# Cross-attention on one core: seven products for three more batches, softmax sums accumulated by ScalarE

## The chip, the cores and the metric

The kernel runs on one core of a Trainium2 chip. Its engines work side by side, each on its own queue in order: TensorE (PE) multiplies matrices and writes PSUM, VectorE (DVE), ScalarE (ACT) and GpSimd (POOL) work on tiles of 128 partitions, and SyncE (SP) issues the transfers. The metric is the time of one execution on the device, in microseconds (us); lower is better.

## The reference

There are 16 batches of 256 queries of width 256 (`x`) and 77 keys of width 192 (`ctx`), 8 heads of width 256, all in fp32. What is computed:

```python
Q = (x @ Wq).reshape(B, -1, 8, 256).transpose(0, 2, 1, 3)
K = (ctx @ Wk)...; V = (ctx @ Wv)...             # the same shape, 77 keys
attn = softmax(where(mask, Q @ K^T / 16, -inf))  # over the 77 keys
out = concat_heads(attn @ V) @ Wo + x
return (out - mean) / sqrt(var + 1e-5) * gamma + beta   # layer norm over 256
```

## The kernel before, in words

The projections are folded into the weights. A first part (to 56.67 us) forms G = Wq Wk^T and U = Wv Wo for each head. After that queries and values are never projected: scores are x times `a` = G ctx^T, and the output is the softmax weights times `vw` = ctx U.

The main loop runs over `b` from -1 to 14. Each turn takes in a new batch (`new`, b + 1), finishes the attention of `now` (b), and normalises and stores `old` (b - 1). A batch is two tiles of 128 queries. The order on each engine is written out by hand in the loop body; no scheduler changes it. In a turn:

- TensorE: `scores` of the new batch (L313, two tiles, two PSUM banks each), `prepare_vw` of the new batch (L241, L252), `prepare_a` for one of the four places of the next group of four batches (L199, L213; only while there is a next group, that is up to the turn in which batch 11 enters), then the attention of batch b.
- VectorE: `shift` (L328 adds the mask's bias to the scores, L335 takes the negated maximum `top`), later `den` (L348, the sum of the exponentials) and `rden` (L350), the statistics of the old batch (`finish`, L484, L487), `invert` (L502, 1/std), `normalise` (L524, L527), `turn` (L366, turns the weights p in blocks of 32), turning of the next group's x (L175; in the turns in which the third and fourth batch of a group enter), `add_product` (L476, adds the product in PSUM to x).
- ScalarE: `exponential` (L342, eight activations a tile, with `top` as bias), a Sqrt for the standard deviation (`spread`, L495, with a table load), the copies of `vw` and `a` out of PSUM (L859), the copy of the seven products' bank (L452), and a first Exp (L865 or L886) that brings the Exp table back.
- GpSimd: `weigh` (L356, p = e times rden), `differences` (L392), `add_seven` (L462), `sums` (L409 to L412), and for tiles that are put `aside` part of normalising (L506, L521, L522).
- SyncE: stores of each finished batch (L535), loads of the next group's x.

The attention of a batch, two tiles of weights times `vw`, is a product of 2 x 2 blocks for the first 64 keys. For batches 0 to 10 (`NS = B - GB - 1`, which is 11) it is done with seven products in place of eight (`seven`, L429): GpSimd forms `differences` of the blocks of vw and `sums` of the blocks of turned p beforehand, TensorE multiplies, and `add_seven` adds the products up. For batches 11 to 15 it is done directly (`attend`, L378). The remaining 13 keys are an ordinary product in both. The branch at L862 takes the seven products, L883 the direct attention of batches 11 to 13 (there the first of two tiles is normalised aside, on ScalarE and GpSimd), L892 that of batch 14; what follows the loop is batch 15.

PSUM has eight banks, given out in rotation; a bank is free again when VectorE or ScalarE has read it. The tiles `s` and `e` have two buffers each, `ts` and `ss` two, turned p four, `vw` three.

Of the kernel before, what the change touches and what calls it, by code (L numbers as in the profile page):

```python
# [8 lines left out]
F32 = mybir.dt.float32  # L9
I32 = mybir.dt.int32  # L10
AF = mybir.ActivationFunctionType
ALU = mybir.AluOpType
AX = mybir.AxisListType
PSUM = bass.MemoryType.PSUM

P = 128
H = 8
D = 256
EPS = 1e-05
GB = 4  # L20
# [33 lines left out]
def kernel(  # L54
# [13 lines left out]
    nc = tc.nc  # L68
    B, S, DI = x.shape
# [4 lines left out]
    NG = B // GB  # L74
# [3 lines left out]
    NF = H // 2  # L78
# [18 lines left out]
    st = ctx.enter_context(tc.tile_pool(name="st", bufs=4))  # L97
# [4 lines left out]
    eps = const.tile([P, 1], F32, tag="eps", name="eps")  # L102
# [6 lines left out]
    NH = DI // 2 // BK  # L109
    uA = const.tile([P, 5, NH, NF, BK], F32, tag="uA", name="uA")  # L110
    uB = const.tile([P, 5, NH, NF, BK], F32, tag="uB", name="uB")
    NS = B - GB - 1

    def of_e(u, e):
        return u[:, 3 - 2 * e : 5 - 2 * e].rearrange("p q n i c -> p (q n) i c")
# [10 lines left out]
    bias = const.tile([P, B, S2], F32, tag="bias", name="bias")  # L126
# [45 lines left out]
    def transpose_x(g, j):  # L172

        cols = xT_of[g][:, j * NM : (j + 2) * NM]
        nc.vector.transpose(cols, cols)  # L175
# [161 lines left out]

    def exponential(t):
        e = sp.tile([P, H, S2], F32, tag="e", name=f"e_{t}")
        s, top = s_of.pop(t)  # L340
        for h in range(H):
            nc.scalar.activation(e[:, h], s[:, h], AF.Exp, bias=top[:, h : h + 1])  # L342
        e_of[t] = e

    def weigh(t):
        e = e_of.pop(t)
        den = st.tile([P, H], F32, tag="den", name=f"den_{t}")
        nc.vector.tensor_reduce(den, e, AX.X, ALU.add)  # L348
        rden = st.tile([P, H], F32, tag="rden", name=f"rden_{t}")
        nc.vector.reciprocal(rden, den)  # L350
        p = p_ring[t % 2]
        e_mh = e.rearrange("p (m h) k -> p m h k", h=2)
        rden_mh = rden.rearrange("p (m h) -> p m h", h=2)
        for cols, keys in ((slice(2 * KM), slice(KM)), (slice(2 * KM, 2 * S2), slice(KM, None))):
            part = p[:, :, cols].rearrange("p m (h k) -> p m h k", h=2)
            nc.gpsimd.tensor_tensor(  # L356
                part,
                e_mh[:, :, :, keys],
                rden_mh.unsqueeze(3).to_broadcast(list(part.shape)),
                ALU.mult,  # L360
            )

    def turn(t):
        p = p_ring[t % 2]
        pT_of[t] = turned.tile([P, NF + 1, NM, BK], F32, tag="pT", name=f"pT_{t}", bufs=4)
        nc.vector.transpose(  # L366
            pT_of[t].rearrange("p n m q -> p m n q"),
            p.rearrange("p m (n k) -> p m n k", k=BK),
        )

    ps_of, s_of, e_of, pT_of, po_of = {}, {}, {}, {}, {}
# [13 lines left out]
        po_of[t] = po  # L385


    def differences(b):

        vw = vw_of[b].rearrange("p q k d -> p q (k d)")  # L390
        ts = vwp.tile([P, 3, 2, P], F32, tag="ts", name=f"ts_{b}", bufs=2)
        nc.gpsimd.tensor_tensor(  # L392
            ts.rearrange("p q k d -> p q (k d)"),
            vw[:, 1:4],
            vw[:, 0:1].to_broadcast([P, 3, 2 * P]),
            ALU.subtract,
        )
        ts_of[b] = ts
# [75 lines left out]
    def add_product(t):  # L474
        y = xg_of[t // GT][:, t % GT, :]
        nc.vector.tensor_tensor(y, po_of.pop(t), y, ALU.add)  # L476

    def finish(t):
        if t in po_of:
            add_product(t)  # L480
        g, j = t // GT, t % GT
        y = xg_of[g][:, j, :]
        bn = st.tile([P, 6], F32, tag="bn", name=f"bn_{t}")
        nc.vector.bn_stats(bn, y)  # L484
        if j == 0:
            mv_of[g] = st.tile([P, GT, 2], F32, tag="mv", name=f"mv_{g}", bufs=2)
        nc.vector.bn_aggr(mv_of[g][:, j, :], bn)  # L487
# [3 lines left out]
    def spread(first, last):  # L491

        g, lo, hi = first // GT, first % GT, (last - 1) % GT + 1
        std = st.tile([P, GT], F32, tag="std", name=f"std_{first}")
        nc.scalar.activation(std[:, lo:hi], mv_of[g][:, lo:hi, 1], AF.Sqrt, bias=eps)  # L495
        std_of[first, last] = std

    def invert(first, last, aside=()):

        g, lo, hi = first // GT, first % GT, (last - 1) % GT + 1  # L500
        rstd = st.tile([P, GT], F32, tag="rstd", name=f"rstd_{first}")
        nc.vector.reciprocal(rstd[:, lo:hi], std_of.pop((first, last))[:, lo:hi])  # L502
        if aside:
            less = st.tile([P, GT], F32, tag="less", name=f"less_{first}")
            for j in (t % GT for t in aside):
                nc.gpsimd.tensor_scalar(  # L506
                    less[:, j : j + 1], mv_of[g][:, j, 0:1], rstd[:, j : j + 1], -1.0,
                    ALU.mult, ALU.mult,
                )
        for t in range(first, last):  # L510
            j = slice(t % GT, t % GT + 1)
            rstd_of[t] = rstd[:, j], less[:, j] if aside else None

    def normalise(t, aside=False):

        g, j = t // GT, t % GT
        rstd, less = rstd_of.pop(t)
        y = xg_of[g][:, j, :]
        if aside:
            nc.scalar.activation(y, y, AF.Identity, bias=less, scale=rstd)  # L520
            nc.gpsimd.tensor_tensor(y, y, gam, ALU.mult)  # L521
            nc.gpsimd.tensor_tensor(y, y, bet, ALU.add)  # L522
        else:
            nc.vector.scalar_tensor_tensor(  # L524
                y, y, mv_of[g][:, j, 0:1], gam, ALU.subtract, ALU.mult
            )
            nc.vector.scalar_tensor_tensor(y, y, rstd, bet, ALU.mult, ALU.add)  # L527
        if t >= NT - QT:
            nc.sync.dma_start(out_rows[:, t, :], y)
            return  # L530
        done.append(t)
        if t ^ 1 in done:
            t |= 1
            j |= 1
            nc.sync.dma_start(  # L535
                out_rows[:, t + 1 - QT : t + 1, :], xg_of[g][:, j + 1 - QT : j + 1, :]
            )
# [291 lines left out]
    for b in range(-1, B - 1):  # L829
        old = range(max(b - 1, 0) * QT, b * QT)  # L830
        now = range(max(b, 0) * QT, (b + 1) * QT)
        new = range((b + 1) * QT, (b + 2) * QT)
        for t in new:
            scores(t)
        for t in new:
            shift(t)
        for n in range(0, 2) if b < 0 else range(b + 2, min(b + 3, B // 2)):
            turn_last(n)
        g, n = (b + 1) // GB + 1, (b + 1) % GB
        work = [prepare_vw(b + 1)]  # L840
        if g < NG:
            work.append(prepare_a(g, (n,)))
            if n == 0:
                load_xT(g)
                load_x(g)
        for part_A, _, _ in work:
            part_A()
        for _, part_B, _ in work:
            part_B()
        for i, t in enumerate(new):  # L850
            exponential(t)
            if old:
                finish(old[i])
            weigh(t)
        if old:
            spread(old[0], old[-1] + 1)
        for _, _, copies in work:
            for dst, src in copies():
                nc.scalar.copy(dst, src)  # L859
        if b + 1 < NS:  # L860
            differences(b + 1)
        if b < NS:  # L862
            if now:
                seven(b)
            nc.scalar.activation(warm, eps, AF.Exp)  # L865
            if old:
                invert(old[0], old[-1] + 1)
                normalise(old[0])
            for t in new:
                turn(t)  # L870
            if n >= NF - 2:
                for j in range((n - NF + 2) * GT // 2, (n - NF + 3) * GT // 2, 2):
                    transpose_x(g, j)
            if old:
                normalise(old[1])
            if now:
                add_seven(b)
            if b + 1 < NS:
                sums(b + 1)
            continue  # L880
        for t in now:
            attend(t)
        if b < B - 2:  # L883
            invert(old[0], old[-1] + 1, aside=old[:1])
            normalise(old[0], aside=True)
            nc.scalar.activation(warm, eps, AF.Exp)  # L886
            turn(new[0])
            normalise(old[1])
            turn(new[1])
            for t in now:  # L890
                add_product(t)
        else:  # L892
            turn(new[0])
            invert(old[0], old[-1] + 1, aside=old)
            for t in old:
                normalise(t, aside=True)
            turn(new[1])
            for t in now:
                finish(t)
            spread(now[0], now[-1] + 1)  # L900


    for t in new:
# [43 lines left out]
```

## Time and profile before

| | |
|---|---|
| median of 3 runs | 282.15 us (280.95 to 282.51) |
| the profiled execution | 280.93 us, span 279.2 us, mean TensorE clock 0.993 |
| busy PE / DVE / ACT / POOL | 269.7 / 206.0 / 166.4 / 168.2 us |
| exponentials L342 | 256 of 346 ns, 67.1 us busy |
| sums of exponentials L348 | 32 of 772 ns, 24.7 us |
| differences L392 on GpSimd | 11 of 1995 ns, 21.9 us |
| main loop begins, last product ends | 56.67 us, about 271.9 us |

How to read it: the span goes from the first to the last instruction of the profiled execution; the rest of that execution's time lies around it. Rows of groups give busy time and the mean of one; neighbours on an engine overlap, so the busy time of a group can be less than its count times its mean. "Idle before" names what released the engine after it had stood still. The chain is the work that ended last, followed back from the last instruction.

### The profile page before, as it was taken

How to read it: one execution, taken by the hardware profiler on the slowest of the kernel's cores; microseconds unless marked ns; L12 is line 12 of the kernel's file. 1: busy time of each engine (PE TensorE's matmuls, PEld its weight loads, DVE VectorE, ACT ScalarE, POOL GpSimd, SP SyncE). 2: the span in 40 equal slices, each digit the busy share in tenths (PEclk: the TensorE clock that was granted, in tenths of full speed). 3: DMA queues.
4: the chain of work that ended last, by engine and by line, in shares of the span. 5: the costliest groups of instructions: out<-in, count | busy, mean ns of one | idle time of the engine just before them, and what ended most of it. 6: DMA issues, size and time to landing. Idle time of an engine off the chain costs nothing.

```text
span 279.2 us, 13274 instructions
## 1 busy us (share of the span) xinstructions
PE 269.7 (97%) x5924; PEld 194.8 (70%) x5924; DVE 206.0 (74%) x421; ACT 166.4 (60%) x447; POOL 168.2 (60%) x228
## 2 busy tenths in 40 slices
PE   8899999999999999999999999999999999999990
PEld 7756599976495959595959585858686858476550
DVE  0353953777738989878788888787787878788873
ACT  2303222146738586868676767777776766978751
POOL 1000069947677777787877777777778445426183
PEclk9999999999999999999999999999999999999997
DMA  6997999920000101940100009501001011010112
GB/s 198 247 223 154 305 262 236 225 82 4 2 6 2 40 5 41 190 155 4 42 2 30 16 25 190 172 5 42 4 5 40 2 42 38 4 41 2 40 39 77
DMA packets 35641, 22.61 MB, mean 81 GB/s; under 512 B 17712, under 2 KB 34048, under 8 KB 35584
## 3 DMA queue, kind: packets, MB, share of 16 engines
q1 hardware_dynamic: 35584, 21.77, 31.1%
q8 instruction: 46, 0.75, 1.2%
q14 instruction: 11, 0.09, 0.1%
HBM read 17.57 MB, written 4.19 MB: 78 GB/s over the span
## 4 chain that ended last, share of the span: by engine, by line
PE 88%; DMA 3%; POOL 2%; ACT 2%; DVE 1%; SPq 1%; issue 0%; ACTq 0%; POOLq 0%
PE ps L313 23%; PE pa L199 12%; PE pv L241 9%; PE po L429 9%; PE pm L429 7%; PE pa L213 6%; PE pv L252 5%; PE po L378 5%; DMA c_sb<-in_ctx_dram 3%; PE pu L676 3%; PE pr L274 2%; ACT e L342 1%; PE pw L690 1%; PE pgb L676 1%; PE pr L284 1%; PE pc L653 1%
## 5 line engine op out<-in xcount | busy, mean ns | idle before, releaser
L342 ACT ACTIVATE e<-s,top 128x77 f32<-128x77 f32 x256 | 67.1, 346 | 52.1 <-DVE top L335 49.9
L356 POOL TENSOR_TENSOR p<-e,rden 128x512 f32<-128x512 f32 x64 | 45.9, 739 | 46.7 <-DVE rden L350 46.4
L313 PE MATMUL ps<-a,xT 128*32 128x154 f32 x2048 | 70.0, 294 | 0.0
L313 PEld LDWEIGHTS ps<-a,xT 128*32 128x32 f32 x2048 | 66.1, 110 | 1.7 <-issue 0.8
L328 DVE TENSOR_TENSOR s<-ps,bias 128x308 f32<-128x308 f32 x64 | 30.3, 474 | 17.7 <-PE ps L313 15.9
L199 PE MATMUL pa<-cA,gA 128*32 128x308 f32 x512 | 35.8, 423 | 0.0
L462 POOL TENSOR_TENSOR xg<-xg,m 128x256 f32<-128x256 f32 x33 | 24.2, 732 | 13.5 <-DVE xg L476 11.8
L199 PEld LDWEIGHTS pa<-cA,gA 128*32 128x32 f32 x512 | 16.4, 110 | 20.9 <-issue 8.0
L241 PE MATMUL pv<-uA,cA 128*32 128x512 f32 x256 | 30.4, 592 | 0.0
L366 DVE STREAM_TRANSPOSE pT<-p 128x640 f32<-128x640 f32 x32 | 25.6, 824 | 2.4 <-POOL p L356 2.4
L348 DVE TENSOR_REDUCE den<-e 128x8 f32<-128x616 f32 x32 | 24.7, 772 | 3.4 <-ACT e L342 3.4
L335 DVE TENSOR_REDUCE top<-s 128x8 f32<-128x616 f32 x32 | 25.5, 795 | 1.1
L664 POOL COPY cB<-cB 64x224 f32<-64x224 f32 (+1 forms) x6 | 1.9, 359 | 35.2 <-DVE cB L153 35.2
L392 POOL TENSOR_TENSOR ts<-vw 128x768 f32<-128x768 f32 x11 | 21.9, 1995 | 0.0
L213 PE MATMUL pa<-cB,gB 64*32 64x308 f32 x512 | 19.5, 420 | 0.0
L378 PE MATMUL po<-vw,pT 128*32 128x256 f32 x320 | 19.2, 380 | 0.0
L859 ACT COPY vw<-pv 128x512 f32<-128x512 f32 x32 | 16.9, 579 | 2.5 <-PE pv L252 2.5
L495 ACT ACT_TABLE_LOAD x14 | 18.0, 1283 | 0.3
L213 PEld LDWEIGHTS pa<-cB,gB 64*32 64x32 f32 x512 | 9.7, 107 | 11.3 <-issue 7.6
L252 PE MATMUL pv<-uB,cB 64*32 64x512 f32 x256 | 17.4, 601 | 0.0
L524 DVE SCALAR_TENSOR_TENSOR xg<-xg,mv,gam 128x256 f32<-128x256 f32 x25 | 17.1, 683 | 0.0
L378 PEld LDWEIGHTS po<-vw,pT 128*32 128x32 f32 x320 | 10.0, 110 | 9.5 <-DVE den L348 2.5
(114 smaller groups left out, 444.9 us busy)
## 6 DMA issues: line engine op xcount, KB each, us to landing
xT<-in_x_dram SPq DMA_DIRECT2D x16, 256.0 KB, 6.2
xg<-in_x_dram SPq DMA_DIRECT2D x4, 1024.0 KB, 7.9
out_dram<-xg SPq DMA_DIRECT2D x15, 256.0 KB, 2.3
wo<-in_L_xattn_Wo_dram SPq DMA_DIRECT2D x4, 512.0 KB, 6.2
wvT<-in_L_xattn_Wv_dram SPq DMA_DIRECT2D x16, 96.0 KB, 3.0
wq_nat<-in_L_xattn_Wq_dram SPq DMA_DIRECT2D x2, 512.0 KB, 5.9
wq_blk<-in_L_xattn_Wq_dram SPq DMA_DIRECT2D x8, 128.0 KB, 5.1
wk_blk<-in_L_xattn_Wk_dram SPq DMA_DIRECT2D x8, 96.0 KB, 5.6
```

The lines of the kernel that those rows point to most:

```text
L199: nc.tensor.matmul(flat(o[i * BK : (i + 1) * BK]), gA[:, h, cols(dc, i)], flat(cA[:, batches, :]), start=not B_first, stop=B_first,)
L213: nc.tensor.matmul(flat(banks[j + k][i * BK : (i + 1) * BK]), gB[half(k), h % NF, cols(dc, i)], flat(cB[half(k), batches, :]), start=B_fir ...
L241: nc.tensor.matmul(pv[k][i * BK : (i + 1) * BK], cA[:, b, k * BK : (k + 1) * BK], uA[:, parts, :, i], start=True, stop=False,)
L252: nc.tensor.matmul(pv[k][i * BK : (i + 1) * BK], cB[half(k), b, k * BK : (k + 1) * BK], uB[half(k), parts, :, i], start=False, stop=True,)
L313: nc.tensor.matmul(ps[m // 2][i * BK : (i + 1) * BK, m % 2 * 2 * S2 : (m % 2 + 1) * 2 * S2], xT_of[g][:, j * NM + m, dc], flat(a_of[g][:, ...
L328: nc.vector.tensor_tensor(s[:, a * H // 2 : (a + 1) * H // 2], ps[a][:, : H // 2 * S2].rearrange("p (h k) -> p h k", k=S2), bias[:, b, :]. ...
L335: nc.vector.tensor_reduce(top, s, AX.X, ALU.max, negate=True)
L342: nc.scalar.activation(e[:, h], s[:, h], AF.Exp, bias=top[:, h : h + 1])
L356: nc.gpsimd.tensor_tensor(part, e_mh[:, :, :, keys], rden_mh.unsqueeze(3).to_broadcast(list(part.shape)), ALU.mult,)
L366: nc.vector.transpose(pT_of[t].rearrange("p n m q -> p m n q"), p.rearrange("p m (n k) -> p m n k", k=BK),)
L378: nc.tensor.matmul(po[i * BK : (i + 1) * BK], pT[:, n, i], vw_of[b][:, 2 - n // 2 * 2 : 4 - n // 2 * 2, n % 2, :] if n < NF else vr[:, b, ...
L429: nc.tensor.matmul(out[i * BK : (i + 1) * BK], weight[:, i], moving, start=(n == 0), stop=(n == len(terms) - 1),)
```

## The change

Three edits.

1. `NS` becomes `B - 2` = 14: the batches 11, 12 and 13 go through `seven`, `add_seven` and `sums` as the earlier ones do, and the branch for them with direct attention and one tile put aside goes away. In those turns ScalarE copies the products, GpSimd adds them and forms the sums, and both tiles of the old batch are normalised on VectorE.
2. The exponentials write the sum over their 77 keys as a second output (`accum_out`), one for each head; VectorE's reduction is gone.
3. `differences` takes the engine: GpSimd as before while there is a next group (batches 0 to 11), VectorE for batches 12 and 13, there behind the turning of p and ahead of the second tile's normalising. The turning of the next group's x gets the condition that there is a next group.

```diff
-    NS = B - GB - 1
+    NS = B - 2
...
     def exponential(t):
         e = sp.tile([P, H, S2], F32, tag="e", name=f"e_{t}")
+        den = st.tile([P, H], F32, tag="den", name=f"den_{t}")
         s, top = s_of.pop(t)
         for h in range(H):
-            nc.scalar.activation(e[:, h], s[:, h], AF.Exp, bias=top[:, h : h + 1])
-        e_of[t] = e
+            nc.scalar.activation(
+                e[:, h], s[:, h], AF.Exp, bias=top[:, h : h + 1], accum_out=den[:, h : h + 1]
+            )
+        e_of[t] = e, den
 
     def weigh(t):
-        e = e_of.pop(t)
-        den = st.tile([P, H], F32, tag="den", name=f"den_{t}")
-        nc.vector.tensor_reduce(den, e, AX.X, ALU.add)
+        e, den = e_of.pop(t)
         rden = st.tile([P, H], F32, tag="rden", name=f"rden_{t}")
...
-    def differences(b):
+    def differences(b, engine):
...
-        nc.gpsimd.tensor_tensor(
+        engine.tensor_tensor(
...
-        if b + 1 < NS:
-            differences(b + 1)
+        if g < NG:
+            differences(b + 1, nc.gpsimd)
         if b < NS:
...
-            if n >= NF - 2:
+            if g < NG and n >= NF - 2:
                 for j in range((n - NF + 2) * GT // 2, (n - NF + 3) * GT // 2, 2):
                     transpose_x(g, j)
+            if g == NG and b + 1 < NS:
+                differences(b + 1, nc.vector)
             if old:
                 normalise(old[1])
...
-        if b < B - 2:
-            invert(old[0], old[-1] + 1, aside=old[:1])
-            normalise(old[0], aside=True)
-            nc.scalar.activation(warm, eps, AF.Exp)
-            turn(new[0])
-            normalise(old[1])
-            turn(new[1])
-            for t in now:
-                add_product(t)
-        else:
-            turn(new[0])
...
+        turn(new[0])
```

More of the change, by code (lines that the diff above doesn't have):

```diff
@@ L882 @@
             attend(t)
-        if b < B - 2:
-            invert(old[0], old[-1] + 1, aside=old[:1])
-            normalise(old[0], aside=True)
-            nc.scalar.activation(warm, eps, AF.Exp)
-            turn(new[0])
-            normalise(old[1])
-            turn(new[1])
-            for t in now:
-                add_product(t)
-        else:
-            turn(new[0])
[L894 to L900, printed above, removed]
+        turn(new[0])
+        invert(old[0], old[-1] + 1, aside=old)
+        for t in old:
+            normalise(t, aside=True)
+        turn(new[1])
+        for t in now:
+            finish(t)
+        spread(now[0], now[-1] + 1)
     for t in new:
```

## The prediction

> **What bounds the kernel now.** I read the page first (busy shares, the chain that ended last), then the chain in order of time, the timeline of the 14.1 us in which batch 10 enters, that of the last 57 us, and the groups by shape.
>
> ```profile
> PE 269.7 (97%) x5924; PEld 194.8 (70%) x5924; DVE 206.0 (74%) x421; ACT 166.4 (60%) x447; POOL 168.2 (60%) x228
> ...
> PE 88%; DMA 3%; POOL 2%; ACT 2%; DVE 1%; SPq 1%; issue 0%; ACTq 0%; POOLq 0%
> ```
>
> TensorE is busy 97% of the span and 88% of the chain. In order of time the chain is TensorE alone, without a gap, from 56.67 to 258.36 us. There TensorE works off one batch per period: 14.10 us (scores start at 193.88 and 207.99), and 11.37 us after batch 11, when no products for a later group are left (scores at 233.46 and 244.84). So it looks as if any product saved is time saved. But there is a second closed loop, which the chain hides because it is just short enough. The timeline shows it (start us, us, engine, line, group; in brackets the idle time before), ScalarE first:
>
> ```profile
> 197.47 4.20 ACT L342 ACTIVATE e<-s,top 128x77 f32<-128x77 f32 x16 [3.52 <-DVE top L335]
> 201.69 1.28 ACT L495 ACT_TABLE_LOAD   x1
> 202.98 0.30 ACT L495 ACTIVATE std<-mv,eps 128x2 f32<-128x2 f32 x1
> 203.19 1.05 ACT L859 COPY vw<-pv 128x512 f32<-128x512 f32 x2
> ...
> 211.57 4.20 ACT L342 ACTIVATE e<-s,top 128x77 f32<-128x77 f32 x16 [3.52 <-DVE top L335]
> ```
>
> and VectorE behind it:
>
> ```profile
> 203.31 0.17 DVE L502 RECIPROCAL rstd<-std 128x2 f32<-128x2 f32 x1 [0.58 <-ACT std L495]
> 203.39 0.81 DVE L524 SCALAR_TENSOR_TENSOR xg<-xg,mv,gam 128x256 f32<-128x256 f32 x1
> 204.24 0.48 DVE L527 SCALAR_TENSOR_TENSOR xg<-xg,rstd,bet 128x256 f32<-128x256 f32 x1
> 204.65 1.57 DVE L366 STREAM_TRANSPOSE pT<-p 128x640 f32<-128x640 f32 x2
> 206.13 1.26 DVE L175 STREAM_TRANSPOSE xT<-xT 128x512 f32<-128x512 f32 x2
> 207.32 0.57 DVE L524 SCALAR_TENSOR_TENSOR xg<-xg,mv,gam 128x256 f32<-128x256 f32 x1
> 207.93 0.48 DVE L527 SCALAR_TENSOR_TENSOR xg<-xg,rstd,bet 128x256 f32<-128x256 f32 x1
> 208.33 0.74 DVE L476 TENSOR_TENSOR xg<-po,xg 128x256 f32<-128x256 f32 x2
> 209.10 0.48 DVE L328 TENSOR_TENSOR s<-ps,bias 128x308 f32<-128x308 f32 x1
> 210.15 0.48 DVE L328 TENSOR_TENSOR s<-ps,bias 128x308 f32<-128x308 f32 x1 [0.57 <-PE ps L313]
> 210.66 0.80 DVE L335 TENSOR_REDUCE top<-s 128x8 f32<-128x616 f32 x1
> ```
>
> Read it in a circle: top of batch 10 releases the exponentials; ScalarE's queue then holds the Sqrt table load and `std`; VectorE waits 0.58 us for `std` and, in order, normalises one tile, turns p, turns blocks of the next group's x (only while batches 2, 3 of a group enter), normalises the second tile (207.32 to 208.33), adds the products, and only then can reach the shift and top of batch 11, which release the next exponentials. From 197.47 to 211.57 one turn takes 14.10 us, and in it VectorE waits for TensorE only 0.57 us. Its own work is 14.10 - 0.57 = 13.53 us with the transposes of x, and 13.53 - 1.26 = 12.27 us without. The covers are thus 0.57 and 1.83 us a turn: this, not TensorE's 97%, prices the change.
>
> ```profile
> L342 ACT ACTIVATE e<-s,top 128x77 f32<-128x77 f32 x256 | 67.1, 346 | 52.1 <-DVE top L335 49.9 <-POOL ss L410 2.2
> ...
> L348 DVE TENSOR_REDUCE den<-e 128x8 f32<-128x616 f32 x32 | 24.7, 772 | 3.4 <-ACT e L342 3.4
> ```
>
> **What the Trainium skill says.** "ScalarE: Activation LUTs", section What ACT_TABLE_LOAD costs: an ACTIVATE with a pointer bias takes about 280 ns + 0.833 ns per element, 186 without a pointer operand, and neighbours overlap by 93 ns. For 77 elements that is 344 ns and one every 251 ns; the trace agrees, 346 ns a row and 4.20/16 = 0.262 us from one to the next. Its 1283 ns table load is the trace's 1.28 us; the drain of 1380 ns that it adds is not to be seen, `std` follows at once. It has no price for the accumulator. "VectorE: DVE Perf Modes", section Two Vector instructions with no wait between them, says of VectorE that an operation which writes its accumulator is two instructions, the second a read; no trace here shows that for ScalarE, and I take it over as an assumption.
>
> **The change part by part.**
>
> Seven products for batches 11 to 13: the two direct attentions take 4.46 us on TensorE (L378 in the chain), seven products and remainders 1.88 + 2.18 = 4.06. Three times 0.40: 1.2 us less TensorE.
>
> Sums on VectorE (L348) removed: 32 x 0.77 = 24.7 us of VectorE. Worth nothing on the loop: the last sum of the turn shown ends at 202.5 and its reciprocal at 202.73, while VectorE then waits for `std` until 203.28. That wait only becomes longer.
>
> Accumulation by ScalarE: 256 times d. The trace has no such row. From below d = 0, if the engine writes the sum along; a gain is excluded, as nothing is taken off ScalarE. From above, the smallest activation of the trace, `warm` with 0.207 us, not overlapped at all. Between lies an instruction without pointer operand that overlaps: by that page 186 ns fixed less the 93 ns overlap, d = 0.093 us, an estimate. I take that: 16 x 0.093 = 1.49 us on every turn, ahead of table load, `std`, the copies of VW and of a, and all that VectorE does behind `std`.
>
> Differences of batches 12, 13 on VectorE: behind the turning of p, inside the loop. GpSimd's row is 1.995 us (L392); on VectorE 256 elements take 0.411 us (L476) and 616 take 0.795 (L335), a line that gives 0.96 us for 768. Bounds 0.8 and 1.1. I take 0.95.
>
> Order in those three turns: before, one of two normalisations is put aside to ScalarE and GpSimd, one turning comes before the other, and nothing else stands there; that turn just fits 11.37 us (VectorE waits 0.54 us for TensorE at 235.62). Now both normalisations are on VectorE, with both turnings before the second one. GpSimd gets five adds and four sums (about 3.3 + 3.0 us a batch) in place of 1.8 us; it has waits of 5.5 us there before p, so I cost this at nothing; without that cover p, then its turning, would be late. ScalarE copies the products m (0.59 us) in place of 0.60 us. No transfer is added, and the stores stand in the same order.
>
> The sum. Turn with x transposes: 13.53 + 1.49 = 15.02, 0.92 over TensorE's 14.10. Without: 12.27 + 1.49 = 13.76, 0.34 under. From the top of batch 2, where normalising begins, to that of batch 12 there are six of the first kind and four of the second: 6 x 0.92 - 4 x 0.34 = 4.16 us late. Up to then TensorE hardly stands still: the sums ss are ready 4 us before use (their last ends at 214.2, TensorE takes them at 218.4), the copies of a some 2.3 us (219.6 against 221.9, scores of batch 12), and the latter run out first. Then the turns of the batches 12 and 13 are 12.27 + 0.95 + 1.49 = 14.71 and that of 14 is 13.76, in all 43.18 us, where the three took 34.13 before (top at 224.76 and 258.89). Batch 15's top is 4.16 + 43.18 - 34.13 = 13.21 us late. What follows is serial:
>
> ```profile
> 265.50 1.05 ACT L859 COPY vw<-pv 128x512 f32<-128x512 f32 x2
> ...
> 267.41 1.91 PE L378 MATMUL po<-vw,pT 128*32 128x256 f32 x32
> ```
>
> The copies of VW end at 266.55, the last attention starts on TensorE at 267.41: 0.86 us of cover. They now come 13.21 + 1.49 late, so TensorE ends 13.84 us later, and with it the kernel; TensorE's 1.2 us are lost in its waiting. On the profiled execution (span 279.2, itself 280.93): 294.8. The median of the three runs is 282.15, 1.2 us above it, which gives **296.0 us**.
>
> **The rivals.**
>
> Accumulation free (d = 0): turns up to batch 12 fit as before. The last three are 13.22, 13.22 and 12.27 = 38.71 against 34.13: 4.58 late, less 0.86: +3.7, 285.9 us. For it: the sum could leave with the activation. Against: the two-instruction reading above.
>
> Read not overlapped (d = 0.186, the page's fixed time in full, to 0.207, `warm`): every turn is over 14.10; with 0.207, 16 x 0.207 = 3.31, 6 x 2.74 + 4 x 1.48 = 22.4 late at batch 12, then 2 x 16.53 + 15.58 - 34.13 = 14.5, then 3.31 - 0.86: +39, 321 us; with 0.186 the same sum gives +35, 317 us. ScalarE then starts to follow its own queue without its waits of 3.5 us for top.
>
> The other side: TensorE still sets the end, as the chain says now, and its 1.2 us come through: 281.0 us. For it: 97% busy, VectorE with 26% idle and 24.7 us taken off. It decides if a turn of the last stage is at most the 10.97 us that TensorE then needs; I count 13.2 even with d = 0, so some 2.2 us of VectorE's or ScalarE's work would have to lie beside other work that my row sum puts in line. That the change does not do what it says is excluded: in the changed program the exponentials have two outputs, L348 is gone, and seven products stand in TensorE's order up to batch 13.
>
> **How the numbers follow.** Forecast (d from 0.05 to 0.13) 0.46; free or nearly so 0.20; not overlapped 0.26; TensorE sets the end 0.06; the remaining 0.02 something that balances. 0.5% (1.4 us) is about what a measurement can tell from no change. All first three are slower: slower 0.92, same 0.02, faster 0.06. The range goes from the free case with the difference at 0.8 us (2 x 0.15 less, 285.5, put at 285) to d = 0.19 (318).
>
> **What would show it.** The exponentials of a tile pair: 5.7 us instead of 4.20. Period of the scores: first 14.1, then longer from group to group, 14 to 15 in the last stage. TensorE waiting for a copies at batch 12, then before the second of the seven products (ss from GpSimd, behind the adds of products). VectorE waiting for `std` longer, and never for ps in the last stage. The forecast is wrong if exponentials still take 4.2 us (then +3.7), or if VectorE still waits for scores in the last stage (then faster).

## The result and the profile after

| | before | after |
|---|---|---|
| median | 282.02 us (4 runs, 280.95 to 282.51) | 290.96 us (4 runs, 289.27 to 292.0) |
| ratio to before, 95% interval | | 1.0317 (1.0285 to 1.035): slower |
| profiled execution, span | 280.93, 279.2 us | 292.0, 290.2 us |
| mean TensorE clock | 0.993 | 0.984 |

The forecast was 296.0 us with a range of 285 to 318. The sign and the main mechanism came as forecast, and the loss of 8.9 us is about two thirds of the forecast 13.8.

The page of after, its busy shares, its chain by engine, and three rows of its groups (count, busy us, mean ns, then the idle time just before with its releaser):

```profile
PE 271.4 (94%) x6116; PEld 200.0 (69%) x6116; DVE 180.1 (62%) x397; ACT 187.2 (64%) x703; POOL 179.1 (62%) x247
...
PE 64%; ACT 14%; DVE 12%; DMA 4%; POOL 2%; issue 2%; SPq 1%; ACTq 0%; DVEq 0%; POOLq 0%
...
L343 ACT ACTIVATE e<-s,top 128x77 f32<-128x77 f32 x256 | 88.0, 346 | 49.3 <-DVE top L335 40.7
...
L343 ACT ACTIVATION_READ_ACCUMULATOR e<-s,top 128x1 f32 x256 | 47.9, 187 | 0.0
...
L351 DVE RECIPROCAL rden<-den 128x8 f32<-128x8 f32 x32 | 6.4, 199 | 39.2 <-ACT e L343 39.2
```

TensorE's share of the chain falls from 88% to 64%, ScalarE's rises from 2% to 14% and VectorE's from 1% to 12%: the second loop is now the one that ends last. ScalarE has a kind of row that the program before did not have, 256 reads of the accumulator of 187 ns each. VectorE, with 24.7 us of reductions gone, waits 39.2 us for exponentials before its reciprocals.

ScalarE's timeline in the turn in which batch 11 enters (start us, us, engine, line):

```profile
214.69 0.36 ACT L343 ACTIVATE e<-s,top 128x77 f32<-128x77 f32 x1 [2.81 <-DVE top L335]
214.96 0.19 ACT L343 ACTIVATION_READ_ACCUMULATOR e<-s,top 128x1 f32 x1
215.05 0.35 ACT L343 ACTIVATE e<-s,top 128x77 f32<-128x77 f32 x1
215.30 0.19 ACT L343 ACTIVATION_READ_ACCUMULATOR e<-s,top 128x1 f32 x1
...
220.10 0.19 ACT L343 ACTIVATION_READ_ACCUMULATOR e<-s,top 128x1 f32 x1
220.30 1.28 ACT L496 ACT_TABLE_LOAD   x1
221.60 0.30 ACT L496 ACTIVATE std<-mv,eps 128x2 f32<-128x2 f32 x1
```

The read starts 0.09 us before its activation ends, and the next activation 0.1 us before the read ends. An activation comes every 0.34 to 0.36 us. From the first one (214.69) to the table load (220.30) the sixteen pairs take 5.61 us.

VectorE's timeline, one turn of the last stage, from the top of batch 13 to that of batch 14:

```profile
241.94 0.80 DVE L335 TENSOR_REDUCE top<-s 128x8 f32<-128x616 f32 x1
...
248.47 0.20 DVE L351 RECIPROCAL rden<-den 128x8 f32<-128x8 f32 x1 [2.03 <-ACT e L343]
250.08 0.17 DVE L503 RECIPROCAL rstd<-std 128x2 f32<-128x2 f32 x1 [1.40 <-ACT std L496]
250.16 0.47 DVE L525 SCALAR_TENSOR_TENSOR xg<-xg,mv,gam 128x256 f32<-128x256 f32 x1
250.67 0.48 DVE L528 SCALAR_TENSOR_TENSOR xg<-xg,rstd,bet 128x256 f32<-128x256 f32 x1
251.07 1.56 DVE L367 STREAM_TRANSPOSE pT<-p 128x640 f32<-128x640 f32 x2
252.56 0.92 DVE L393 TENSOR_TENSOR ts<-vw 128x768 f32<-128x768 f32 x1
253.39 0.47 DVE L525 SCALAR_TENSOR_TENSOR xg<-xg,mv,gam 128x256 f32<-128x256 f32 x1
253.90 0.48 DVE L528 SCALAR_TENSOR_TENSOR xg<-xg,rstd,bet 128x256 f32<-128x256 f32 x1
254.31 0.75 DVE L477 TENSOR_TENSOR xg<-po,xg 128x256 f32<-128x256 f32 x2
254.97 0.85 DVE L328 TENSOR_TENSOR s<-ps,bias 128x308 f32<-128x308 f32 x2
255.86 0.80 DVE L335 TENSOR_REDUCE top<-s 128x8 f32<-128x616 f32 x1
```

From one top to the next, in the circle that the prediction describes: 241.94 + 13.92 = 255.86. VectorE waits 1.40 us for `std` (0.58 before), and the two shifts (L328) run back to back in 0.85 us: it never waits for scores here. TensorE waits instead, as its timeline shows (the bracket is the idle time before the row, with what ended it):

```profile
242.91 0.64 PE L430 MATMUL pm<-vw,pT 128*32 128x128 f32 x16
245.48 0.65 PE L430 MATMUL pm<-vw,ss 128*32 128x128 f32 x16 [1.93 <-POOL ss L412]
...
259.37 0.65 PE L430 MATMUL pm<-vw,ss 128*32 128x128 f32 x16 [2.70 <-POOL ss L412]
...
260.73 1.10 PE L430 MATMUL po<-vw,pT 128*32 128x128 f32 x16
...
277.55 1.99 PE L379 MATMUL po<-vw,pT 128*32 128x256 f32 x32 [1.43 <-ACT vw L860]
```

It stands for `ss` in two of the three last turns, and before the last attention for the copies of VW. None of these waits sets the loop, because VectorE finds the scores ready. They are what the late loop leaves for TensorE.

Where the 11.0 us between the two spans lie, by the start of the first tile's top (L335):

| stretch | before | after | difference |
|---|---|---|---|
| start to the top of batch 2 | 83.75 | 85.62 | +1.87 |
| top of batch 2 to top of batch 12 | 141.01 | 142.40 | +1.39 |
| top of batch 12 to top of batch 15 | 34.13 | 40.89 | +6.76 |
| top of batch 15 to the end | 20.31 | 21.29 | +0.98 |

The first row is not the change. In the ten experiments below this point lies anywhere from 83.87 to 85.55; three of them have the code of after up to there, and they have 83.87, 84.31 and 84.67. In after the chain ahead of the loop holds the load of ctx with 10.23 us, where before has 8.35: 1.88 us, the whole row, in a load that the change doesn't touch. The other three rows sum to 9.13, close to the 8.94 between the medians.

### The profile page after: what moved, and what is told of

Same layout as the page of the kernel before. It is cut to its first block, busy times and chain, and to the rows that moved or that the text cites. A ratio compares the mean times of both kernels' runs of the same rounds, so it can differ in the third digit from the quotient of the medians.

```text
span 290.2 us, 13888 instructions
## 1 busy us (share of the span) xinstructions
PE 271.4 (94%) x6116; PEld 200.0 (69%) x6116; DVE 180.1 (62%) x397; ACT 187.2 (64%) x703; POOL 179.1 (62%) x247
## 4 chain that ended last, share of the span: by engine, by line
PE 64%; ACT 14%; DVE 12%; DMA 4%; POOL 2%; issue 2%; SPq 1%; ACTq 0%; DVEq 0%; POOLq 0%
PE ps L313 15%; ACT e L343 11%; PE pa L199 10%; PE po L430 7%; PE pv L241 6%; PE pm L430 6%; PE pa L213 5%; DMA c_sb<-in_ctx_dram 4%; PE pv L252 4%; PE pu L677 3%; DVE pT L367 3%; ACT L496 2%; PE pr L274 2%; DVE top L335 2%; DVE xg L528 2%
## 5 line engine op out<-in xcount | busy, mean ns | idle before, releaser
L343 ACT ACTIVATE e<-s,top 128x77 f32<-128x77 f32 x256 | 88.0, 346 | 49.3 <-DVE top L335 40.7
L357 POOL TENSOR_TENSOR p<-e,rden 128x512 f32<-128x512 f32 x64 | 44.1, 711 | 32.4 <-DVE rden L351 32.4
L343 ACT ACTIVATION_READ_ACCUMULATOR e<-s,top 128x1 f32 x256 | 47.9, 187 | 0.0
L463 POOL TENSOR_TENSOR xg<-xg,m 128x256 f32<-128x256 f32 x42 | 30.9, 735 | 16.8 <-DVE xg L477 14.2
L328 DVE TENSOR_TENSOR s<-ps,bias 128x308 f32<-128x308 f32 x64 | 29.1, 472 | 8.8 <-PE ps L313 6.8
L351 DVE RECIPROCAL rden<-den 128x8 f32<-128x8 f32 x32 | 6.4, 199 | 39.2 <-ACT e L343 39.2
L393 POOL TENSOR_TENSOR ts<-vw 128x768 f32<-128x768 f32 x12 | 22.1, 1843 | 9.5 <-ACT vw L860 9.5
L335 DVE TENSOR_REDUCE top<-s 128x8 f32<-128x616 f32 x32 | 25.5, 795 | 1.1
L430 PE MATMUL po<-vr,pT 128*32 128x128 f32 x448 | 20.5, 278 | 0.0
L463 POOL TENSOR_TENSOR m<-m 128x128 f32<-128x128 f32 x28 | 13.9, 496 | 5.4 <-ACT m L453 4.3
```

What stands on the lines that cost most here:

```text
L328: nc.vector.tensor_tensor(s[:, a * H // 2 : (a + 1) * H // 2], ps[a][:, : H // 2 * S2].rearrange("p (h k) -> p h k", k=S2), bias[:, b, :]. ...
L335: nc.vector.tensor_reduce(top, s, AX.X, ALU.max, negate=True)
L357: nc.gpsimd.tensor_tensor(part, e_mh[:, :, :, keys], rden_mh.unsqueeze(3).to_broadcast(list(part.shape)), ALU.mult,)
L430: nc.tensor.matmul(out[i * BK : (i + 1) * BK], weight[:, i], moving, start=(n == 0), stop=(n == len(terms) - 1),)
L463: nc.gpsimd.tensor_tensor(to, to, what, ALU.add)
```

## The experiments

The theory ahead of the runs: the closed loop (top, exponentials, `std`, VectorE's work, the next top) became longer than TensorE's period, mostly in the last three turns, by the reads of the accumulator and by what the two other edits put on VectorE there. The rivals: the reads cost on every turn from the start; or the loss comes from the new order of the last stage or from GpSimd and not from ScalarE.

**Each edit alone.** First all but the accumulation (VectorE's sums put back):

```diff
-            nc.scalar.activation(
-                e[:, h], s[:, h], AF.Exp, bias=top[:, h : h + 1], accum_out=den[:, h : h + 1]
-            )
+            nc.scalar.activation(e[:, h], s[:, h], AF.Exp, bias=top[:, h : h + 1])
...
         e, den = e_of.pop(t)
+        nc.vector.tensor_reduce(den, e, AX.X, ALU.add)
```

> Seven products for batches 11 to 13 and differences of 12, 13 on VectorE, but the sums of exponentials by VectorE as before. Loop theory (the turn exponentials, std, normalise, turn, shift has become longer than TensorE's period in the last stage): the turns there lose the 1.39 us of the accumulator reads, 13.92 becomes about 12.5 to 12.9, still over 10.97, so +2.3 to +3.5 us against before: 284.3 to 285.5. Rival 1 (the reads cost by themselves, wherever they stand): without them only TensorE's gain is left, about 281. Rival 2 (GpSimd's sums and adds for the three batches are late, VectorE's loop is not the cause): nearly all of the loss stays, 289 to 291.

Measured: 286.09 us, ratio 1.0155 (1.0116 to 1.0194). Up to batch 12 every turn is 14.10; the last three are 12.87, 12.79 and 11.91. So the seven products, which take 1.2 us off TensorE, cost 4.2 us by themselves: both normalisations and the differences now stand on VectorE in line. ScalarE's sixteen exponentials in this kernel, with the second tile's top ready in time:

```profile
240.34 4.11 ACT L343 ACTIVATE e<-s,top 128x77 f32<-128x77 f32 x16 [4.11 <-DVE top L335]
244.47 1.28 ACT L495 ACT_TABLE_LOAD   x1
```

240.34 to 244.47 is 4.13 us, where after has 5.61: 1.48 / 16 = 0.0925 us per accumulated activation, the estimate of 0.093 almost to the digit. In the turns before, where the second tile waits a little for its top, the same step is 4.22, and the difference 1.39.

Then the accumulation alone, on the kernel before:

```diff
+        den = st.tile([P, H], F32, tag="den", name=f"den_{t}")
...
-            nc.scalar.activation(e[:, h], s[:, h], AF.Exp, bias=top[:, h : h + 1])
-        e_of[t] = e
+            nc.scalar.activation(
+                e[:, h], s[:, h], AF.Exp, bias=top[:, h : h + 1], accum_out=den[:, h : h + 1]
+            )
+        e_of[t] = e, den
...
-        nc.vector.tensor_reduce(den, e, AX.X, ALU.add)
```

> The kernel before with the accumulating exponentials alone. Loop theory: turns of the last stage go from 11.37 to about 12.2 (10.8 of own work + 1.39), three times 0.8, and 0.5 to 1.0 in the tail: 285 to 286. Rival 1: the whole of after's loss and TensorE's 1.2 us on top, about 292. Rival 2: no change, 282.

Measured: 285.65 us, ratio 1.0145 (1.0108 to 1.0183). The last three turns are 12.14, 12.12 and 12.11 in place of 11.37. Each by itself, the edits cost 4.2 and 3.8 us, together 8.9. (From batch 2's top on the two traces hold 3.3 and 3.8 of it; the other 0.9 of the first lies in the start, which scatters.) In a turn: before, VectorE waits 0.54 for scores in the last stage, so its own turn is 10.83; the products bring it to 12.79 (+1.96), the accumulation to 12.12 (+1.29), both to 13.92 (+3.09). The work adds up almost plainly, and the cover of 0.54 is spent only once.

**Where the accumulation costs.** After, accumulating only in batches 0 to 11 (VectorE sums the rest):

```diff
+            if t < NT - 4 * QT:
...
+        if not (t < NT - 4 * QT):
+            nc.vector.tensor_reduce(den, e, AX.X, ALU.add)
```

> The changed kernel, with accumulation for batches 0 to 11 only; sums by VectorE for 12 to 15. Loop theory: the reads of the early batches lie in cover (turns of 14.24 and 13.0 against TensorE's 14.10), so the time is that of seven products alone within 0.7 us: 284.5 to 286. Rival 1: three quarters of the reads are there, so three quarters of after's loss, about 289. Rival 2: 289 to 291.

Measured: 286.18 us, ratio 1.0161 (1.0128 to 1.0194), the same as with no accumulation at all (286.09). Its turns with the transposes of x are 14.23 to 14.24; the two that follow in each group, 13.83 and 14.10, win it back, since TensorE's scores still come every 14.10: 14.24 + 14.23 + 13.83 + 14.10 = 56.40, four times TensorE's 14.10. Only the last group's 0.27 stay.

And only in batches 12 to 15:

```diff
+            if NT - 4 * QT <= t:
...
+        if not (NT - 4 * QT <= t):
+            nc.vector.tensor_reduce(den, e, AX.X, ALU.add)
```

> The changed kernel, with accumulation for batches 12 to 15 only; sums by VectorE for 0 to 11. Loop theory: all of after's loss is still there, 290 to 291. Rival 1: a quarter of the reads, 283 to 284. Rival 2: 289 to 291 as well (told apart by the two runs before).

Measured: 289.46 us, ratio 1.028 (1.0237 to 1.0323), with turns of 14.10 up to batch 12 and then 13.92, 13.92 and 13.04, those of after to 0.01. The rival that the reads cost on every turn falls: in the first twelve batches alone they make no difference that these runs show (286.18 against 286.09), in the last four 3.4 us (289.46 - 286.09). The two don't add up to after, which took 1.5 us more than this run. In after's trace 1.40 us more lie between the tops of batch 2 and batch 12, and 1.1 of them come from the one turn of batch 8 to 9, which the run before this one, with the same early reads, doesn't have. That turn comes up again below; its cause stays open.

**What the last loop is made of.** If work in line between `std` and the shift is what costs, moving it behind the next shift must give it back. In the last stage the old batch is inverted and normalised behind the shift of the next turn:

```diff
+        if g_of_b(b) > NG and b < B - 1 and held:
+            r = held.pop()
+            invert(r[0], r[-1] + 1)
+            for t in r:
+                normalise(t)
...
-            if old:
+            if old and g == NG:
+                held.append(old)
+            elif old:
                 invert(old[0], old[-1] + 1)
...
-            if old:
+            if old and g < NG:
                 normalise(old[1])
```

> The changed kernel, with the normalising of the old batch in the last stage (batches 10, 11, 12) put behind the next batch's shift on VectorE, so that std is no longer between the exponentials and the next shift. Loop theory: the turns fall to TensorE's period, 10.97 to 11.4 instead of 13.92, and the time to that of before within 1 us (TensorE's 1.2 us gained, about 1 us of reads in the tail lost): 281 to 283. Rival 1 (reads cost by themselves) and rival 2 (GpSimd's sums late): 290 to 291, unchanged.

Measured: 284.81 us, ratio 1.0107 (1.0084 to 1.013). About 6 us of the 8.9 come back, the last turns being 11.53, 12.38 and 10.99, but the 281 to 283 us that I expected were missed. VectorE's timeline of the moved block (the first two and last two rows are one tile each), and GpSimd's at the same time:

```profile
240.67 0.97 DVE L525 SCALAR_TENSOR_TENSOR xg<-xg,mv,gam 128x256 f32<-128x256 f32 x1
241.68 0.83 DVE L528 SCALAR_TENSOR_TENSOR xg<-xg,rstd,bet 128x256 f32<-128x256 f32 x1
242.44 0.95 DVE L525 SCALAR_TENSOR_TENSOR xg<-xg,mv,gam 128x256 f32<-128x256 f32 x1
243.42 0.48 DVE L528 SCALAR_TENSOR_TENSOR xg<-xg,rstd,bet 128x256 f32<-128x256 f32 x1
```

```profile
240.62 0.74 POOL L411 TENSOR_TENSOR ss<-pT,pT 128x256 f32<-128x256 f32 x1
241.44 0.79 POOL L412 TENSOR_TENSOR ss<-pT,ss 128x256 f32<-128x256 f32 x1
242.31 0.80 POOL L413 TENSOR_TENSOR ss<-pT,ss 128x256 f32<-128x256 f32 x1
```

In after such a pair of rows is 0.47 and 0.48. Here, beside GpSimd's sums, L525 takes 0.97 and 0.95 and L528 once 0.83, and two of GpSimd's three additions go from 0.74 to 0.79 and 0.80. It is always the row that starts second that gets longer: L525 at 240.67 starts behind L411, which keeps its 0.74, and L412 at 241.44 starts while L525 has 0.20 us to go. The block stands in front of `rden`, and through it p and its turning come late in the same turn. The deferral works, but it was put beside GpSimd, at a price that I hadn't counted.

The differences of batches 12 and 13 back on GpSimd:

```diff
-        if g < NG:
+        if b + 1 < NS:
             differences(b + 1, nc.gpsimd)
...
-            if g == NG and b + 1 < NS:
-                differences(b + 1, nc.vector)
```

> The changed kernel, differences of batches 12 and 13 on GpSimd as for the others. Loop theory: two turns lose 0.84 us of VectorE's work, 13.92 becomes 13.08: 1.7 us less than after, 289.3. Rival 2: 2 x 2 us more on GpSimd, so slower than after by up to 4 us, 293 to 295.

Measured: 289.39 us, ratio 1.0273 (1.0247 to 1.03), against the 289.3 of the loop theory. The turns become 13.34, 13.34 and 13.05: 0.58 less where a difference was, not the 0.84 expected, since the second normalisation now starts beside GpSimd's differences (1.84 us) and the add behind them (L525 0.65 and L528 0.57 in place of 0.47 and 0.48). The other expectation, a kernel made slower by more work on GpSimd, is refuted.

One turning of p ahead of the invert, into VectorE's wait for `std`:

```diff
+            if g == NG:
+                turn(new[0])
             if old:
                 invert(old[0], old[-1] + 1)
                 normalise(old[0])
-            for t in new:
+            for t in new[1:] if g == NG else new:
                 turn(t)
```

> The changed kernel, in the last stage the turning of the new batch's first tile put ahead of the reciprocal of std on VectorE, into its wait of 1.41 us for std. Loop theory: 0.75 us less in each of three turns, 13.92 becomes 13.2: 2.2 us less than after, 288.7. Rivals 1 and 2: as after, 291.

Measured: 289.16 us, ratio 1.0266 (1.0233 to 1.03); expected were 288.7. The last turns are 13.51, 13.50 and 12.44, 0.41 to 0.61 shorter. The 1.40 us that VectorE waits can hold work, and what is put there (0.75) comes off the turn, apart from some 0.3 where the differences and the normalising behind them now meet GpSimd's adds (L393 1.02 and L525 0.68 in place of 0.92 and 0.47).

**What the sums on VectorE were worth.** After, with the accumulation kept (its result unused) and VectorE's reduction put back and used:

```diff
+        acc = st.tile([P, H], F32, tag="acc", name=f"acc_{t}", bufs=1)
...
-                e[:, h], s[:, h], AF.Exp, bias=top[:, h : h + 1], accum_out=den[:, h : h + 1]
+                e[:, h], s[:, h], AF.Exp, bias=top[:, h : h + 1], accum_out=acc[:, h : h + 1]
...
         e, den = e_of.pop(t)
+        nc.vector.tensor_reduce(den, e, AX.X, ALU.add)
```

> The changed kernel with the sums twice: the accumulated ones are written and not used, VectorE forms those that are used as before. If the removed reduction is worth nothing on the loop (the prediction's step): turns stay at 14.24 and 13.92, 291. If it moves GpSimd's p 0.8 us later, into the first normalising, whose rows get 0.36 us longer beside it: turns of 14.6 and 14.3, some 2 to 3.5 us more than after, 293 to 294.5.

Measured: 296.12 us, ratio 1.0513 (1.049 to 1.0536): about 5 us more than after, where 293 to 294.5 in all were expected. The prediction had called the removal of the sums worth nothing on the loop. GpSimd's p of the second tile, in the last stage of this kernel, and VectorE's rows at that time:

```profile
237.56 1.56 POOL L359 TENSOR_TENSOR p<-e,rden 128x512 f32<-128x512 f32 x2 [1.56 <-DVE rden L353]
```

```profile
238.00 0.17 DVE L505 RECIPROCAL rstd<-std 128x2 f32<-128x2 f32 x1 [0.58 <-ACT std L498]
238.08 0.81 DVE L527 SCALAR_TENSOR_TENSOR xg<-xg,mv,gam 128x256 f32<-128x256 f32 x1
238.93 0.48 DVE L530 SCALAR_TENSOR_TENSOR xg<-xg,rstd,bet 128x256 f32<-128x256 f32 x1
```

The reduction delays `rden` and so p, which then runs beside the first normalisation. L527 takes 0.81 us, and from `rstd` to the turning of p pass 1.33 us (238.00 to 239.33), where after has 0.99. Every turn with the transposes of x goes from 14.24 to 14.78, and the turns of the last stage get longer by as much (13.92 to 14.47). Of these 0.54 us, 0.35 are this step. The other 0.20 are ScalarE's: the sixteen pairs take 5.81, not 5.61, with a pause between the two tiles that I put down to the single buffer of `acc`. So the removed sums were worth about 0.35 us a turn, not nothing; the 0.20 belong to the experiment.

**A version that wins?** Two combinations, both built on after. The first has accumulation only from batch 12 on, puts the differences behind the next shift, and the held normalising between the two reciprocals of the next turn:

```diff
+            if NT - 4 * QT <= t:
...
+        if B - GB <= b < NS:
+            differences(b, nc.vector)
...
+            if i == 1 and True:
+                deferred()
             weigh(t)
...
-            if old:
+            late = g == NG
+            if late:
+                held.append(old)
+            elif old:
...
```

> Accumulation for batches 12 to 15 only; in the last stage the normalising of the old batch is put between the two reciprocals of the sums (where VectorE waited 2.03 us for the exponentials), and the differences behind the next batch's shift. Against the run with the normalising behind the shift (284.8): nothing stands ahead of GpSimd's p, so the turns should be TensorE's, 11.0 to 11.4 (there 11.53, 12.38, 10.99). Loop theory: 281.0 to 282.5, that is before within 0.5%; the 1.2 us of TensorE are gained and about as much is lost in the tail, where the reads stand in line. Rival 1: 283 or more (a quarter of the reads). Rival 2: as the changed kernel with late accumulation, 289.

Measured: 283.13 us, ratio 1.0064 (1.005 to 1.0077). TensorE's timeline, the scores of the batches 12 to 15 and the last attention's wait:

```profile
222.98 4.37 PE L313 MATMUL ps<-a,xT 128*32 128x154 f32 x128
...
233.97 4.37 PE L313 MATMUL ps<-a,xT 128*32 128x154 f32 x128
...
245.13 4.37 PE L313 MATMUL ps<-a,xT 128*32 128x154 f32 x128
...
256.44 4.37 PE L313 MATMUL ps<-a,xT 128*32 128x154 f32 x128
...
268.71 1.99 PE L384 MATMUL po<-vw,pT 128*32 128x256 f32 x32 [0.71 <-ACT vw L877]
```

The first of these periods is 10.99 us, what TensorE needs with seven products (the prediction had 10.97). The next two are 11.16 and 11.31, so TensorE takes 33.46 us for three, where before takes 11.37 for each. But the tops follow at 10.99, 11.94 and 11.31, 34.24 in all against 34.13: VectorE, with rows of up to 1.34 us for the differences and 1.16 for L533 beside GpSimd, lets the gain go. At the end TensorE stands for the copies of VW, and from batch 15's top to the end it takes 21.4 us (260.08 to 281.5), where before needs 20.3. Nearly all of this goes with the reads: the six other runs of this document that accumulate in batch 15 and don't sum it again take 21.2 to 21.3 there, and the two that don't accumulate it and leave the normalising in its place take 20.2. The held normalising, which now stands ahead of the last reciprocal, adds 0.2 at most.

The second leaves batch 15 out of the accumulation and puts the last held normalising at the end of the last turn, ahead of its Sqrt:

```diff
-            if NT - 4 * QT <= t:
+            if NT - 4 * QT <= t < NT - QT:
...
-            if i == 1 and True:
+            if i == 1 and b < B - 2:
                 deferred()
...
+        deferred()
         spread(now[0], now[-1] + 1)
```

> The same with accumulation for batches 12 to 14 only and the last held normalising at the end of the last turn. Loop theory: as the run beside it, and the tail keeps VectorE's sums as before: 281 to 282.

Measured: 283.53 us, ratio 1.0084 (1.0069 to 1.0098). Its tail is longer still, 21.8 us, where the runs without reads in batch 15 have 20.2: here it is the held normalising that stands in line, from 270.70 to 273.18 ahead of the next batch's `rstd`. Both miss what I expected (281 to 282.5 and 281 to 282), and no version that I ran beats before. With the turns at TensorE's period the end hangs on what is left for VectorE, ScalarE and GpSimd after batch 15's top.

## Why the prediction was right, and where its sizes were off

- **The bound** (the second loop and not TensorE's 97%): right. Accumulation and products each lengthen that loop, TensorE's 1.2 us end in its waits for `ss` and `vw`, and the loop's share of the chain rises as said. The rival in which TensorE still sets the end would have shown turns of 10.97; they were 13.92.
- **The accumulator** (d = 0.093, bounds 0 and 0.207): right, 0.087 to 0.0925 by the step measured. That the accumulator is read by a second instruction, which the prediction took over as an assumption from the Trainium skill, "VectorE: DVE Perf Modes", section Two Vector instructions with no wait between them, holds for ScalarE in this trace: 256 rows of its own. Its price was an analogy with another instruction; that it fits so well no run here explains. Both end cases, free and not overlapped, are refuted by the timeline.
- **Differences on VectorE** (0.95): 0.92 a row, and 0.83 from its start to the next one's, as neighbours overlap.
- **Sums removed, worth nothing on the loop**: this step failed. It asked only what VectorE had waited for next, not where the earlier `rden` would move GpSimd's p. In the kernel before, the second p lies over the first normalisation, which is the L524 row of 0.81 us at 203.39 shown in the prediction. GpSimd's timeline of before and of after (the turn shown above):

```profile
202.88 1.56 POOL L356 TENSOR_TENSOR p<-e,rden 128x512 f32<-128x512 f32 x2 [0.44 <-DVE rden L350]
```

```profile
248.76 1.38 POOL L357 TENSOR_TENSOR p<-e,rden 128x512 f32<-128x512 f32 x2 [1.18 <-DVE rden L351]
```

  Before, p runs from 202.88 to 204.44, over that row. After, it ends at 250.14, and L525 starts at 250.16 and takes 0.47. The step from `rstd` to the turning of p is 1.34 before and 0.99 after. The Trainium skill, "SBUF — State Buffer", section Who interferes with whom, says that a DVE instruction with two SBUF inputs contends with a GpSimd instruction that reads SBUF. The traces agree for `normalise` (both inputs in SBUF), and `add_product`, which takes one input from PSUM, keeps its 0.74 us for two beside GpSimd's sums of products in the run with the differences moved back. The section calls what the two share an exclusive lock, and the traces fit that too. p is two instructions, seen one by one here, the first two rows from before and the last from after:

```profile
202.88 1.05 POOL L356 TENSOR_TENSOR p<-e,rden 128x512 f32<-128x512 f32 x1 [0.44 <-DVE rden L350]
203.89 0.55 POOL L356 TENSOR_TENSOR p<-e,rden 128x104 f32<-128x104 f32 x1
...
249.77 0.37 POOL L357 TENSOR_TENSOR p<-e,rden 128x104 f32<-128x104 f32 x1
```

  In before L524 starts at 203.39, half a microsecond before the first row ends, and is 0.34 longer than L525 in after. The second row starts 0.31 before L524 ends (204.20) and is 0.18 longer than alone. So each waits for what is left of the row that started before it, less 0.13 to 0.19 us; L525 and L412 of the deferral give the same (0.69 left and 0.50 longer, 0.20 left and 0.05 longer). In before's own last stage, where a turning stands between `rstd` and L524, L524 takes 0.44.
- **The turn's own work** (15.02 with transposes of x, 14.71 in the last stage): measured 14.24 and 13.92. The 0.79 less in the latter: 0.35 by the step just told, 0.12 by the differences, 0.10 by the exponentials, 0.09 by the second normalisation (1.01 to 0.92), and 0.11 and 0.10 by the adds and shifts (0.77 to 0.66, 0.99 to 0.89); against these, 0.08 that the prediction took off too much with the transposes of x and by rounding. The last two I read as waits for scores too short for the timeline to name: the cover was some 0.2 larger than the 0.57 in its bracket. The rows shown agree with it: in after the first shift starts 0.09 us before the adds end (254.97 against 254.31 + 0.75), in the kernel before 0.03 us behind their end (209.10 against 208.33 + 0.74), and a bracket counts only from the end of the row ahead. No run tests it.
- **4.16 us late at batch 12**: 1.39. The turns with transposes are over by 0.14 and not 0.92, and the next turns win that back, so that only the last group's 0.28 remain. The other 1.11 come from one turn, batch 8 to 9, 14.92 in place of 13.82, in which TensorE stands still in the middle of the scores:

```profile
182.83 3.46 PE L313 MATMUL ps<-a,xT 128*32 128x154 f32 x97 [0.67 <-issue]
```

  With so little lateness the copies of a at batch 12 stayed in time, and the forecast wait for them is not there.
- **9.05 us in the last stage**: 6.76, all of the difference being the turn's size (0.79 + 0.79 + 0.71). **0.63 in the tail**: 0.98.
- **GpSimd's added work, at nothing**: right. TensorE waits for its `ss`, but the loop does not.

Sum: 1.39 + 6.76 + 0.98 = 9.13 for the 13.84 forecast. Most of what a turn was over-sized by is the step on the sums and the cover read 0.2 too small, 0.56 of the 0.79, and it was carried through each turn; the turn of batch 8 to 9, which nothing in the forecast stands for, takes 1.1 us of the difference back.

## What to carry to other kernels

When one engine looks saturated, look for the closed loop that the chain hides, and price a change by that loop's slack; a row taken off an engine that waits can still pay or cost, by where it moves the engines that it feeds. A sum that rides on an activation isn't free: on ScalarE here it costs 0.09 us each, in line. And where work can be moved into a wait, ask what GpSimd does in that moment.

## What the runs showed of the hardware that I had not expected

- A `scalar_tensor_tensor` of 128x256 on VectorE, 0.44 to 0.48 us alone, takes 0.81 to 0.97 when it starts during a GpSimd `tensor_tensor`, 0.57 when little of that is left, and 1.16 (in the first of the last two versions) behind a p that is held up itself. GpSimd's instructions get longer in the same way: by 0.06 where VectorE was nearly done, by 0.18 in p, and by 0.60 (0.73 to 1.33) behind the differences on VectorE in that version.
- After TensorE had waited 2.70 us for `ss`, its mean granted clock was 0.66 from 260 to 265 us, and 0.50 from 260.8 to 264.0: sixteen of its products took 1.10 us (260.73 above), which take 0.62 elsewhere. After the wait of 1.93 us, 14 us earlier, they took 0.62. No threshold follows from this: with the differences on GpSimd a wait of 2.14 us was followed by such a stretch (0.50 from 258.9 to 262.2), with the accumulation alone one of 2.42 us was not (1.00 from 270.7 to 275.4). In after the scores that followed were still in time for VectorE, so it cost nothing.
- The standstill of TensorE in the scores of batch 9 has no releaser in the trace. The turn of batch 8 to 9 is 14.92 in after, 14.98 and 15.19 in the deferral and with differences on GpSimd, where the same turn one group earlier takes 13.82. With the accumulation alone, one turning first, both sums and the first of the last two versions it is 14.15 to 14.55, 0.1 to 0.7 more than one group earlier. It isn't lengthened at all in the kernel before, with all but the accumulation, with the accumulation only early or only late, and in the last version. What sets it stays open; it is at most 1.4 us of any result here.
